# Pacing transfers and stages in the plan of a conv-scan-attention kernel on one core

## The chip, the cores and the metric

The kernel runs on one core of a Trainium2 chip. The core has five engines with a queue each, in which instructions run in order: PE (matmuls), DVE (VectorE), ACT (ScalarE), POOL (GpSimd) and SP (SyncE, which here issues all transfers). The metric is the device time of one execution in microseconds (us); lower is better.

## The reference, cut to what matters

Eight images of 384 channels and 32 x 32 pixels (1024 tokens) go through two layers. The first is a Mamba block, run forward and backward over the tokens, beside a local 3 x 3 convolution. The second is causal attention with 6 heads, and a feed-forward layer.

```python
# layer 0, per image; L = 1024 tokens, C = 384 channels, 16 states
u, z  = split(rmsnorm(x) @ in_proj)              # also with tokens reversed
u     = silu(causal_conv4(u) + b)
dt, Bm, Cm = split(u @ x_proj)
delta = softplus(dt @ dt_proj + dt_b)
h[t]  = exp(delta*A)[t] * h[t-1] + (delta*u)[t] * Bm[t]   # scan, C x 16 rows
y     = (sum over states of h*Cm + u*D) * silu(z)
x     = x + res * (scale * (y_fwd + y_bwd) @ out_proj + sigmoid(conv3x3(xn)) * xn)
# layer 1
t = t + attention(layernorm(t));  t = t + ffn(layernorm(t))
```

## The kernel before, in words

**Tiles.** The 384 x 16 scan rows of an image and a direction are cut into groups of 128 rows (8 channels x 16 states). With two directions that is 96 groups, so 96 scans a batch (one image) and 768 in all. A scan step (`group`) has these instructions: SP loads `dA` (512 KB, delta broadcast over the states), ACT takes its exponential (L999), PE spreads delta times u over the rows into a PSUM ring (L323, `ring<-du,dup`), DVE multiplies it with B in two halves (L1028), DVE runs the scan (L1034, `h<-dA,ring`), POOL multiplies h with C (L1038), PE sums over the states (`y<-h,sel`). There are six `dA` and six `h` buffers.

**Stages.** Around the scans of batch b stand the other stages of the neighbouring batches: `project` and `gates` (norm, in_proj; PROJECT), `prepare` (causal convolution and x_proj; CONV), `deltas` (softplus and the splitting of delta times u in three bf16 parts, 39 POOL operations of 1024 columns a batch, L794 and L903 to L918; DELTA), `local` (the 3 x 3 convolution; LOCAL), `finish` (out_proj, layer norm; OUTPUT), `attention` (ATTEND), and `forward` (feed-forward; FORWARD). Their tiles come from one pool of 26 buffers and a PSUM pool of four banks. They pass data by DRAM: `urd`, `xpd`, `ded`, `dusd`, `uzd`, `ygd`, `x1d`.

**Order.** Nothing is in the order of the source. Every operation is recorded in a `Plan` with an engine, a cost, what it reads and writes, and a priority `at`. `Plan.run` then goes through a model of the five engines in time: on each engine it takes, of the operations that could start first, the one with the lowest `at`. It writes out one fixed order for each engine. On the chip the engines follow this order, whatever the real times are.

An operation of a stage gets its `at` from the stage's stretch: `stretch` (L1397) turns, say, DELTA = (-0.82, -0.45) into a window of time around the start of its batch's scans, in units of PERIOD, and `Window` spreads the operations over it; transfers get MOVE less, evictions of PSUM EVICT less. An operation of a scan step is `placed` at its step's time with a lead: LOAD for the dA load, DECAY for the exponential, PRODUCTS for POOL's product, SUMS for PE's sums, PARTS for the load of delta times u. A lead is how much earlier, on the priority scale, the operation ranks than its scan. Operations that have an `at` of their own are `urgent`; in the scans these are all.

In the model a transfer takes its bytes over DMA_RATE, one after the other (`dma` is when the last is through), and DMA_LATENCY more. STAY lowers the `at` of ACT operations that need no change of ACT's function table. The choice:

```python
for t, o in cand:
    if t <= t0 + 0.05:
        a = o.at - (self.STAY if e == "ACT" and o.table in (None, table) else 0.0)
        k = (a, o.index)
```

Of the kernel before, what the change touches and what calls it, by code (L numbers as in the profile page):

```python
# [104 lines left out]
class Plan:  # L105
    LATENCY = 0.06
    SLACK = 0.3
    SWITCH = 1.3
    STAY = 0.0
    DMA_LATENCY, DMA_RATE = 2.5, 280e3  # L110

    def __init__(self, slots):
        self.ops, self.slots = [], slots
# [53 lines left out]
    def run(self):  # L167

        engines = ("PE", "ACT", "DVE", "POOL", "SP")
        free = {e: 0.0 for e in engines}  # L170
        ready = {e: [] for e in engines}
        dma = 0.0
        table = None
        slots = {k: [(0.0, i) for i in range(n)] for k, n in self.slots.items()}

        queue = {k: [] for k in slots}
        for o in self.ops:
            for v in o.allocs:
                if v.kind != "psm":
                    queue[v.kind].append((o.at, o.index, v))  # L180
                    o.waits += 1
        for q in queue.values():
            q.sort(key=lambda a: a[:2])
            q.reverse()
        owner = {}
        for o in self.ops:
            for v in o.allocs:
                owner[id(v)] = o

        def release(o, t):  # L190
            o.ready = max(o.ready, t)
            o.waits -= 1
            if o.waits == 0:
                ready[o.engine].append(o)

        def hand_out(kind):
            while queue[kind] and slots[kind]:
                v = queue[kind].pop()[2]
                t, v.slot = heapq.heappop(slots[kind])
                release(owner[id(v)], t)  # L200

        for o in self.ops:
            if o.waits == 0:
                ready[o.engine].append(o)
        for kind in queue:
            hand_out(kind)
        order = []

        def bank_time(o):

            need = {}
            for v in o.allocs:
                if v.kind == "psm":
                    need[v.kind] = need.get(v.kind, 0) + 1
            t = 0.0
            for k, n in need.items():
                if len(slots[k]) < n:
                    return None
                t = max(t, sorted(slots[k])[n - 1][0])
            return t  # L220

        total = len(self.ops)
        while len(order) < total:
            best = None
            for e in engines:
                cand = []
                for o in ready[e]:
                    t = o.ready
                    if o.allocs:
                        tb = bank_time(o)  # L230
                        if tb is None:
                            continue
                        t = max(t, tb)
                    cand.append((max(t, free[e]), o))
                if not cand:
                    continue
                t0 = min(c[0] for c in cand)

                pick, key = None, None
# [4 lines that stand above are left out]
                        if key is None or k < key:  # L244
                            pick, key, start = o, k, t
                if best is None or start < best[0]:
                    best = (start, e, pick)
            assert best is not None, "the slots do not suffice"
            start, e, o = best
            ready[e].remove(o)  # L250
            for v in o.allocs:
                if v.kind == "psm":
                    _, v.slot = heapq.heappop(slots[v.kind])
            cost = o.cost
            if e == "ACT" and o.table is not None and o.table != table:
                cost += self.SWITCH
                table = o.table
            free[e] = start + cost
            o.done = start + cost + self.LATENCY
            if e == "SP":  # L260
                dma = max(dma, start + cost) + o.nbytes / self.DMA_RATE
                o.done = dma + self.DMA_LATENCY
            order.append((start, len(order), o))
            for u in o.after:
                release(u, start)
            for u in o.users:
                release(u, (o.done if u.engine != e or e == "SP" else free[e]) + (0.0 if u.urgent or u.engine == e else self.SLACK))
            for v in o.vals:
                v.left -= 1
                v.end = max(v.end, o.done)  # L270
                if v.left == 0 and v.kind is not None:
                    heapq.heappush(slots[v.kind], (v.end, v.slot))
                    if v.kind != "psm":
                        hand_out(v.kind)
        order.sort(key=lambda a: a[:2])
        return [o for _, _, o in order]
# [3 lines left out]
def conv_attn_hybrid_kernel(  # L280
# [162 lines left out]

    EVICT, MOVE, SUMS, PRODUCTS, DECAY, LOAD, PARTS = 20.0, 15.0, 30.0, 20.0, 35.0, 45.0, 10.0

    CONV, DELTA, LOCAL, PROJECT = (-0.84, -0.78), (-0.82, -0.45), (-0.51, -0.36), (-1.28, -1.16)
    OUTPUT, ATTEND, FORWARD = (1.04, 1.12), (1.2, 1.85), (1.88, 1.97)

    class Window:

# [939 lines left out]

    PERIOD, HEAD = 475.0, 90.0

    def stretch(span, b):  # L1397
        return Window(span[0] * PERIOD, span[1] * PERIOD, HEAD + b * PERIOD)
# [117 lines left out]
```

## Time and profile before

| | |
|---|---|
| time, median of 3 runs | 4386.56 us (4378.64 to 4395.95) |
| the profiled execution | 4387.34 us, its span 4385.3 us |
| busy | PE 83%, DVE 78%, POOL 68%, ACT 66% of the span |
| DMA | 884.15 MB, mean 202 GB/s |
| table loads | 260, 333.6 us of ACT |
| granted PE clock, mean | 0.888 |

The time around the span is 2 us. Busy shares are averages over stages with different limits, and matmuls are pipelined, so a busy PE is not PE at its peak. "PE s L323" in a wait means: the instruction that wrote tile s, recorded at line 323 (the helper through which most matmuls go). In the prediction, batch n is the stretch from the first scan of image n to the first of image n + 1, and a block is an eighth of it, 12 scans.

### The profile page before, as it was taken

Reading aid. Unit: us, or ns where it says so; the run is one execution under the profiler, and the core shown is the slowest. Engines: PE = TensorE matmul, PEld = TensorE weight load, DVE = VectorE, ACT = ScalarE, POOL = GpSimd, SP = SyncE. Lnnn points to the kernel's source line nnn. Section 1 sums busy time; section 2 is a strip of 40 time slices with the busy share of each in tenths; the row PEclk is TensorE's granted clock in tenths of the full one; section 3 lists DMA queues with packets and bytes.
Section 4 is the critical chain, followed back from the end, with each engine's and each line's share of the span. In section 5 each row is a group of like instructions: output and inputs, shape, how many; then the busy total and the mean of one; then the engine's idle time right before and its main releaser. Section 6 shows DMA issues by size and latency. Waiting matters only on the chain. (4 is left out here: it accounts for less than half of the span.)

```text
span 4385.3 us, 55001 instructions
## 1 busy us (share of the span) xinstructions
PE 3655.8 (83%) x17970; PEld 1442.5 (33%) x17970; DVE 3432.0 (78%) x3661; ACT 2886.3 (66%) x4598; POOL 3000.9 (68%) x2370
## 2 busy tenths in 40 slices
PE   6476668789887899889898899878898888888998
PEld 2021112334233332334333332333323332343363
DVE  1676789879887899869996799879898699999422
ACT  4648436766677758767677767777578666665463
POOL 2967856987579865987569864897559875676231
PEclk8586679889998999889997999979998899999998
DMA  6798995687866788677876879677876757556200
GB/s 214 245 279 252 264 278 170 178 243 213 228 206 201 215 244 246 178 221 219 221 228 181 236 216 253 186 204 226 223 231 179 231 165 197 156 145 171 77 16 25
DMA packets 308918, 884.15 MB, mean 202 GB/s; under 512 B 39080, under 2 KB 92344, under 8 KB 308632
## 3 DMA queue, kind: packets, MB, share of 16 engines
q1 hardware_dynamic: 308632, 880.64, 69.6%
q8 instruction: 143, 2.34, 0.2%
q14 instruction: 143, 1.17, 0.1%
HBM read 709.03 MB, written 173.26 MB: 201 GB/s over the span
## 5 line engine op out<-in xcount | busy, mean ns | idle before, releaser
L1038 POOL TENSOR_TENSOR h<-h,bc 128x1024 f32<-128x1024 f32 x768 | 1810.2, 2362 | 899.2 <-DVE h L1034 735.5
L1034 DVE TENSOR_TENSOR_SCAN h<-dA,ring 128x1024 f32<-128x1024 f32 x768 | 1755.4, 2286 | 164.7 <-PE y L323 64.9
L1028 DVE TENSOR_TENSOR ring<-ring,bc 128x512 f32<-128x512 f32 x1536 | 1071.1, 697 | 331.8 <-PE ring L323 223.0
L999 ACT ACTIVATE dA<-dA,nA 128x1024 f32<-128x1024 f32 x768 | 870.9, 1147 | 584.3 <-DMA dA<-ded 540.6
L323 PE MATMUL ring<-du,dup 32*128 32x512 bf16 x1536 | 327.9, 418 | 404.1 <-DVE h L1034 385.9
L323 PE MATMUL y<-h,sel 128*32 128x512 f32 x3072 | 567.6, 688 | 26.3 <-POOL h L1038 23.2
L1197 DVE TENSOR_REDUCE mx<-s 128x1 f32<-128x512 f32 (+3 forms) x576 | 286.5, 544 | 214.5 <-PE s L323 214.5
L1204 ACT ACTIVATE p<-s,mx 128x512 f32<-128x512 f32 (+3 forms) x576 | 330.4, 579 | 130.6 <-DVE mx L1197 129.3
L1250 POOL TENSOR_SCALAR p<-p,den 128x512 f32<-128x512 f32 (+3 forms) x576 | 328.2, 588 | 113.5 <-DVE den L1243 107.5
L1257 PE MATMUL t<-ident,p 128*128 128x128 f32 x1728 | 304.4, 313 | 117.3 <-POOL p L1250 65.8
L323 PEld LDWEIGHTS <-dup 32*128 32x128 bf16 x1536 | 73.7, 92 | 944.1 <-DVE h L1034 831.7
L1452 ACT ACT_TABLE_LOAD x260 | 333.6, 1283 | 4.7
L1264 ACT COPY pT<-t 128x512 f32<-128x512 f32 (+3 forms) x576 | 253.0, 483 | 124.5 <-PE t L1257 121.8
L323 PE MATMUL s<-k,q 64*128 64x512 f32 (+3 forms) x1152 | 303.5, 579 | 32.5 <-ACT p L1204 30.8
L1257 PEld LDWEIGHTS t<-ident,p 128*128 128x128 f32 x1728 | 216.8, 157 | 269.5 <-POOL p L1250 130.3
L323 PE MATMUL pi<-xp,win 128*128 128x512 f32 x576 | 284.4, 617 | 9.8 <-ACT zt L730 5.7
L323 PE MATMUL pc<-pT,v 128*64 128x128 f32 x3456 | 267.9, 297 | 5.3 <-ACT pT L1264 4.6
L323 PEld LDWEIGHTS pc<-pT,v 128*64 128x64 f32 x3456 | 208.4, 147 | 99.1 <-issue 37.9
L918 POOL TENSOR_TENSOR u<-u,part 128x1024 f32<-128x1024 f32 x96 | 204.6, 2131 | 52.5 <-ACT part L910 52.5
L910 ACT CAST part<-u 128x1024 bf16<-128x1024 f32 x144 | 150.1, 1043 | 57.6 <-DMA dusd<-part 22.7
L323 PEld LDWEIGHTS y<-h,sel 128*32 128x32 f32 x3072 | 88.0, 115 | 289.6 <-issue 146.9
L323 PE MATMUL pg<-yg,wout 128*128 128x512 f32 x288 | 155.8, 658 | 21.0 <-DMA yg<-ygd 18.4
(184 smaller groups left out, 4814.8 us busy)
## 6 DMA issues: line engine op xcount, KB each, us to landing
dA<-ded SPq DMA_DIRECT2D x768, 512.0 KB
ct<-urd SPq DMA_DIRECT2D x96, 513.5 KB
du<-dusd SPq DMA_DIRECT2D x96, 512.0 KB
xs<-xpd SPq DMA_DIRECT2D x96, 432.8 KB
dusd<-part SPq DMA_DIRECT2D x288, 128.0 KB
ded<-de SPq DMA_DIRECT2D x48, 512.0 KB
uz<-uzd SPq DMA_DIRECT2D x48, 512.0 KB
bc<-bcd SPq DMA_DIRECT2D x32, 512.0 KB
```

Source lines behind the costliest of these rows:

```text
L323: return nc.tensor.matmul(out_, lhsT=lhsT, rhs=rhs, start=first, stop=last)
L918: "POOL", pool(L), lambda part=part: nc.gpsimd.tensor_sub(du.t, du.t, part.t), [part], [du]
L999: "ACT", act(L) + 0.1, lambda: nc.scalar.activation(dA.t, dA.t, AF.Exp, scale=nA.t[:, g : g + 1]),
L1028: uses("DVE", nc.vector.tensor_mul(to, to, bc.t[:, 0, half(hf)]), [bank_of(v)])
L1034: i = nc.vector.tensor_tensor_scan(h.t[:, rev], dA.t[:, rev], t[:, rev], 0.0, ALU.mult, ALU.add)
L1038: op("POOL", pool(L), lambda: nc.gpsimd.tensor_mul(h.t, h.t, bc.t[:, 1]), [(bc, 1)], [h], at=at - PRODUCTS)
L1197: lambda sc=sc, g=g, w=k1 - k0, hh=hh: nc.vector.tensor_reduce(mx.t[:, g, hh : hh + 1], sc[hh].t[:, 0:w], AX.X, ALU.max, negate=True), [sc ...
L1204: nc.scalar.activation(ps[hh].t[:, k0:k1], sc[hh].t[:, 0 : k1 - k0], AF.Exp, bias=mx.t[:, g, hh : hh + 1], accum_out=den.t[:, g, hh : hh + 1],
L1250: nc.gpsimd.tensor_scalar(t, t, den.t[:, g, hh : hh + 1], 1.0, ALU.mult, ALU.mult)
L1257: nc.tensor.transpose(t.t[:, j * P - k0 : (j + 1) * P - k0], ps[hh].t[:, j * P : (j + 1) * P], ident)
L1264: nc.scalar.copy(pT[hh].t[:, k0 // P : k1 // P, :].rearrange("p j t -> p (j t)"), t.t[:, 0 : k1 - k0])
L1452: nc.scalar.preload_act_table_set(table)
```

## The change

It changes no computation and no tile. In the model it adds a gate: a transfer that isn't urgent may start only when the transfers under way have no more than BACKLOG = 4 us left. The model's rate of DMA goes from 280 to 262 GB/s, and ACT now prefers by 10 us to stay with its function table (LANDING is 0 and has no effect). The leads PRODUCTS, DECAY, LOAD and PARTS get smaller, PRODUCTS below zero, so that a product ranks after its scan's own time. The stretches of the stages and PERIOD are set anew. Lines of the kernel after line 262 move by four.

```diff
     SWITCH = 1.3
-    STAY = 0.0
-    DMA_LATENCY, DMA_RATE = 2.5, 280e3
+    STAY = 10.0
+    BACKLOG = 4.0
+    LANDING = 0.0
+    DMA_LATENCY, DMA_RATE = 2.5, 262e3
...
                         t = max(t, tb)
+                    if e == "SP" and not o.urgent:
+                        t = max(t, dma - self.BACKLOG)
                     cand.append((max(t, free[e]), o))
...
                 dma = max(dma, start + cost) + o.nbytes / self.DMA_RATE
-                o.done = dma + self.DMA_LATENCY
+                o.done = dma + self.DMA_LATENCY + self.LANDING
...
-    EVICT, MOVE, SUMS, PRODUCTS, DECAY, LOAD, PARTS = 20.0, 15.0, 30.0, 20.0, 35.0, 45.0, 10.0
-
-    CONV, DELTA, LOCAL, PROJECT = (-0.84, -0.78), (-0.82, -0.45), (-0.51, -0.36), (-1.28, -1.16)
-    OUTPUT, ATTEND, FORWARD = (1.04, 1.12), (1.2, 1.85), (1.88, 1.97)
+    EVICT, MOVE, SUMS, PRODUCTS, DECAY, LOAD, PARTS = 20.0, 15.0, 30.0, -10.0, 20.0, 15.0, 5.0
+
+    CONV, DELTA, LOCAL, PROJECT = (-0.93, -0.84), (-0.86, -0.39), (-0.41, -0.29), (-1.31, -1.16)
+    OUTPUT, ATTEND, FORWARD = (1.04, 1.22), (1.23, 1.78), (1.88, 1.97)
...
-    PERIOD, HEAD = 475.0, 90.0
+    PERIOD, HEAD = 420.0, 90.0
```

## The prediction

> **What bounds the kernel now.** I read the page first, then the windows of one batch, then the waits. The busy shares and the two costliest groups of the page:
>
> ```profile
> PE 3655.8 (83%) x17970; PEld 1442.5 (33%) x17970; DVE 3432.0 (78%) x3661; ACT 2886.3 (66%) x4598; POOL 3000.9 (68%) x2370
> ...
> L1038 POOL TENSOR_TENSOR h<-h,bc 128x1024 f32<-128x1024 f32 x768 | 1810.2, 2362 | 899.2 <-DVE h L1034 735.5
> L1034 DVE TENSOR_TENSOR_SCAN h<-dA,ring 128x1024 f32<-128x1024 f32 x768 | 1755.4, 2286 | 164.7 <-PE y L323 64.9
> ```
>
> No engine is full on average, so the averages decide nothing. The 768 scans on DVE are the kernel's clock: one scan and the two products with B before it (L1028, 697 ns each) cost 2.286 + 2 x 0.697 = 3.68 us, and every scan is followed by one product with C on POOL (L1038, 2.36 us). From the scans' start times the span divides into 138.3 us before the first scan, eight batches of 96 scans (494.9, 479.8, 504.2, 505.9, 505.7, 502.3, 517.7, and 445.0 to the end of the last scan), and 291.4 us after it. Batches 2 to 6 repeat one order, so I look at batch 3, cut into eight blocks of 12 scans. These are the windows of the blocks (busy us and instructions of each engine, granted clock, DMA share, GB/s):
>
> ```profile
> core 0: us, PE busy (x) PEld busy (x) DVE busy (x) ACT busy (x) POOL busy (x), PEclk, DMA share, GB/s
> 1617.00:1680.00 63.00, 55.59 (x204) 17.88 (x201) 55.79 (x57) 40.40 (x47) 30.06 (x14) 0.97 0.83 226
> 1680.00:1740.00 60.00, 55.24 (x238) 15.90 (x238) 56.77 (x59) 48.19 (x57) 30.29 (x14) 1.00 0.95 290
> 1740.00:1789.00 49.00, 45.49 (x219) 18.62 (x213) 43.96 (x38) 39.05 (x51) 35.71 (x16) 1.00 0.55 160
> 1789.00:1858.00 69.00, 57.45 (x282) 26.96 (x280) 51.60 (x57) 54.66 (x93) 68.24 (x48) 0.78 0.63 179
> 1858.00:1943.00 85.00, 65.95 (x380) 26.94 (x381) 55.57 (x66) 60.83 (x109) 76.46 (x65) 0.82 0.72 209
> 1943.00:2012.00 69.00, 60.23 (x396) 27.19 (x395) 58.32 (x71) 53.40 (x97) 57.07 (x62) 0.85 0.80 236
> 2012.00:2071.00 59.00, 55.66 (x328) 24.61 (x326) 55.52 (x63) 40.24 (x83) 40.85 (x46) 1.00 0.67 200
> 2071.00:2123.00 52.00, 48.31 (x224) 19.38 (x226) 48.69 (x47) 30.46 (x48) 34.99 (x33) 1.00 0.80 231
> ```
>
> The reader is to see two regimes. In blocks 2, 7 and 8 DVE is busy 93 to 95%: DVE is the bound. In blocks 4 to 6 DVE falls to 75, 65 and 85% while POOL has 99, 90 and 83%: POOL is the bound. What a DVE wait looks like there, the waits of block 5 alone:
>
> ```profile
> DVE mx L1197 <- PE s L323: 14.2, 1, 14.2
> DVE h L1034 <- PE y L323: 4.7, 1, 4.7
> DVE fac L1235 <- POOL fac L1232: 3.8, 1, 3.8
> ```
>
> PE is named, but PE's sums (y) wait for POOL's products, and whatever stands behind them on PE (the scores s) waits too. PE itself isn't full: its matmuls of a batch, each at the spacing that saturated stretches show (430 ns for a pass of 512 fp32 columns), make about 345 of 506 us.
>
> **What the Trainium skill says.** "DMA: Bandwidth & Descriptors" (Queues, rings and completion order; Anatomy of one DMA) says that DMA engines don't wait on semaphores: the issuing sequencer waits before dispatch. So a transfer that must wait holds up all transfers behind it on SP. The trace agrees: SP's queue waits 1405.1 us for scans to free a dA buffer. "ScalarE: Activation LUTs" (What ACT_TABLE_LOAD costs) gives about 1283 ns for a table load; the 260 loads here have a mean of 1283 ns. "Perfetto Trace Analysis" (Optimization Strategy) reads consistent gaps as a possible lack of buffers; here the gap of blocks 4 to 6 repeats in each batch, and h has six buffers.
>
> **The change, part by part.** It adds and removes no work but table loads: the changed program has the same instructions except 251 table loads for 261 (the opening one included). 10 x 1.283 = 13 us of ACT, which has 138 us of slack in each batch (367 of 506 busy): costed at nothing. All else is order. So I gave each instruction of the new order the duration that the same instruction had in this profile, and summed between scans (POOL: between its products). Per batch the sums stay (DVE 443, POOL 382, ACT 402 to 400). Block by block, us, batch 3:
>
> ```
> block          1     2     3     4     5     6     7     8
> measured      62.6  59.8  49.7  68.7  84.7  69.5  58.4  52.4
> DVE  before   57.5  59.3  44.8  53.0  57.8  62.1  57.7  50.4
> POOL before   29.6  29.6  43.1 100.6  57.1  45.4  40.1  36.1
> DVE  after    56.0  53.2  52.5  52.8  55.0  58.4  62.9  51.9
> POOL after    29.6  32.0  63.8  75.8  45.1  59.2  38.8  37.3
> MB   before   14.0  16.1  10.0  12.1  15.2  16.8  13.2  11.9
> MB   after    15.1  13.1  12.6  11.3  11.3  12.9  16.9  15.8
> ```
>
> POOL's peak is the delta stage. Block 4 has 12 products (28.5), 23 delta operations (52.7) and softmax scaling (19.4); in the new order the 39 delta operations of a batch spread over 1, 13, 13, 6 and 6 in blocks 2 to 6 (before: 6, 23 and 10 in blocks 3 to 5). A rule follows from before: **DVE loses about POOL's largest surplus over it in a run of blocks.** Block 4: 100.6 - 53.0 = 47.6; by half blocks, scans 30 to 48: 127.1 - 75.6 = 51.5. Measured: blocks 4 to 6 took 222.9 us for 172.9 of DVE work, a loss of 50.0. After: blocks 3 and 4, 139.6 - 105.3 = 34.3; by half blocks, scans 30 to 66, 201.6 - 158.4 = 43.2. The gain is 8 to 13 us; I take 10. Batches 2 to 6: **-50 us**. What is late next is DVE itself (443 of work in about 496), and ACT in block 5 (67.1 of work).
>
> Batch 1: surplus before, blocks 3 to 5, 193.6 - 155.6 = 38.0 (measured loss of blocks 3 to 6: 40.3); after, 204.9 - 162.4 = 42.5, by half blocks 49.8. **+8 us**.
>
> Batch 0 mixes two bounds: DMA runs at 0.90 with 264 GB/s, and DVE loses 111 us, of which POOL's surplus explains 39 (blocks 1 and 2: 10; 4 and 5: 29). In the order, dA loads stand in its second half only 0.5 to 3.5 scans ahead of their scan; in the new one 3 to 5. 134.6 MB between its first and last dA load become 126.5; batch 1 takes the rest. Against that, POOL's surplus grows to 29 (block 1, 74.0 - 44.9) and 60 (block 5, 114.2 - 54.3). So 384 of DVE work + 89 + about 12 left of other waits = 485: **-10 us**, with -35 and +20 as ends.
>
> Head: the compute engines' order up to the first scan is the same but for two POOL operations. On SP, ten small weight loads (wqkv_2, bvc, w_fc1, w_p1, kr2) move from ahead of the convolution's loads to behind them: 10 issues of 0.5 to 1.2 us, about 7 us; PE waits 19.1 us for wc there. The loads' own 6.9 MB hide some. **-5 us**. The selection of kr2 on POOL waits longer then, but POOL idled 24.6 us after it.
>
> Batch 7 (428 of DVE work in both) and the tail (DVE 78 in both, ACT 162 to 159, PE a few us less): 0 and **-3**.
>
> The gate itself (BACKLOG): a transfer outside the scans is put after more dA loads, and each of these waits for a scan. Behind it wait its stage's first matmul or activation. The trace can't show that delay; above, the earlier windows (CONV from -0.93 instead of -0.84) should pay for it. I bound it by +20 us a batch (the 19.1 us that PE waits for wc in the head) and, since a dA load that finds a shorter queue can also land earlier, by a gain of 6 (the first rival); I take 0. The later priority of POOL's products (PRODUCTS) is in the block sums; its side effect, that sums stand up to six scans behind in more places, costs nothing as long as POOL is the bound there.
>
> Sum: -50 + 8 - 10 - 5 - 3 = -60, against the profiled execution's 4387.3 us: 4327. The median, 4386.6, is 0.7 lower; I say **4326**.
>
> **Rivals.**
> - *The transfers come free* (13%): dA loads are on time in batch 0 (the 111 us of loss become 75) and POOL's surplus costs 16 a batch less. -36 - 80 + 8 - 8: about 4270. For it: the leads of the loads in the new order. Against: block 5 of batch 0 needs 114 us of POOL whatever DMA does.
> - *The stall moves* (18%): products put behind softmax scaling wait for ACT and DVE on the in-order POOL queue, POOL idles in blocks 3 to 6 as it does now (34 us between 1740 and 2012, though 246 of work stand there) and the loss stays at 50. -50 is gone: about 4377.
> - *DMA becomes the bound between batches* (17%), slower: blocks 7, 8 and 1 now carry 39.1 MB in 173.4 us, 225 GB/s; in the new order 47.8 MB in about 176, 272 GB/s. If the queue gives only 245 there, they take 195, 19 us more, and every scan waits for its dA: 5 x (19 - 10) + 8 - 10 - 8, about 4422. It decides below 47.8 MB / 186 us = 257 GB/s. Against it: block 2 now moves 290 GB/s at a share of 0.95 with DVE 95% busy. For it: batch 0 kept no more than 264.
>
> **How the numbers follow.** The forecast (own range 4295 to 4360) has 52%, the rivals 13, 18 and 17. A measurement of this kernel tells about 0.5% (22 us) from no change. Faster by more: 52 + 13 = 0.65; within: 0.18; slower: 0.17. The range 4262 to 4402 takes in the second rival, the ends of batch 0 and half of the slow one.
>
> **What would show it.** Right: in the windows of batch 3 the time of blocks 4 to 6 falls from 223 to about 200 and block 3 grows to some 62; no window has POOL at 0.99 with DVE below 0.7; batches 2 to 6 take about 496; the first scan starts near 133; 250 table loads. The forecast is wrong if blocks 3 to 6 together stay at 272, if ACT's waits on dA's DMA grow beyond 540.6 us with DVE waiting behind them, or if block 5 of batch 0 takes over 130 us.

## The result, and the profile after

| | before | after |
|---|---|---|
| median of 4 runs, us | 4385.08 (4378.64 to 4395.95) | 4320.97 (4314.89 to 4327.89) |
| profiled execution; its span, us | 4387.34; 4385.3 | 4314.89; 4313.2 |
| granted PE clock, mean | 0.888 | 0.90 |

The ratio is 0.9852 (95% interval 0.9823 to 0.988): **faster by 1.5%**, 64 us by the medians. The page of after, its busy shares and the same two groups:

```profile
PE 3641.6 (84%) x17970; PEld 1454.5 (34%) x17970; DVE 3426.9 (79%) x3661; ACT 2871.3 (67%) x4588; POOL 3003.6 (70%) x2370
...
L1042 POOL TENSOR_TENSOR h<-h,bc 128x1024 f32<-128x1024 f32 x768 | 1808.3, 2364 | 887.0 <-DVE h L1038 746.0
L1038 DVE TENSOR_TENSOR_SCAN h<-dA,ring 128x1024 f32<-128x1024 f32 x768 | 1755.3, 2286 | 271.7 <-PE y L327 130.7
```

Work and durations are the same (2286 ns a scan, 2362 and 2364 a product); the shares rose because the span fell. The scan even waits longer for PE's sums (130.7 us against 64.9). From the scans' start times:

| stretch, us | head | b0 | b1 | b2 | b3 | b4 | b5 | b6 | b7 | tail |
|---|---|---|---|---|---|---|---|---|---|---|
| before | 138.3 | 494.9 | 479.8 | 504.2 | 505.9 | 505.7 | 502.3 | 517.7 | 445.0 | 291.4 |
| after | 135.7 | 503.9 | 491.9 | 486.6 | 497.3 | 485.4 | 489.9 | 489.4 | 443.8 | 289.2 |

Batches 2 to 6 gained 87.2 us, batches 0 and 1 lost 21.1, the rest gained 6. The windows of after's batch 3, the same eight blocks of 12 scans (us, busy us and instructions of each engine, granted clock, DMA share, GB/s):

```profile
1618.00:1676.00 58.00, 52.62 (x187) 16.03 (x185) 53.86 (x54) 39.40 (x46) 28.50 (x13) 1.00 1.03 252
1676.00:1738.00 62.00, 56.41 (x257) 15.11 (x256) 51.71 (x50) 52.58 (x59) 30.94 (x15) 0.94 0.97 269
1738.00:1793.00 55.00, 49.73 (x198) 20.71 (x197) 50.85 (x52) 43.01 (x61) 48.40 (x21) 0.98 0.63 187
1793.00:1851.00 58.00, 53.91 (x271) 24.77 (x270) 50.89 (x54) 45.53 (x83) 56.36 (x42) 0.79 0.59 183
1851.00:1921.00 70.00, 60.70 (x384) 33.46 (x382) 52.35 (x61) 51.51 (x97) 67.88 (x61) 0.89 0.55 163
1921.00:1982.00 61.00, 48.72 (x318) 20.15 (x318) 55.34 (x65) 48.90 (x95) 58.35 (x63) 0.86 0.93 261
1982.00:2052.00 70.00, 59.67 (x354) 24.11 (x355) 60.37 (x71) 47.65 (x88) 45.92 (x48) 0.93 0.86 237
2052.00:2115.00 63.00, 59.62 (x289) 24.76 (x289) 49.81 (x49) 34.99 (x58) 37.01 (x34) 1.00 0.73 218
```

Blocks 4 to 6 took 189 us (before 223), but blocks 7 and 8 took 133 (before 111): DVE is now busy 86 and 79% where it had 94% in both. So a large gain in the middle of the batch is partly given back at its end. In batch 4, scans 24 to 72 went from 272.3 to 240.9 us and scans 72 to 96 from 109.8 to 128.4.

### The profile page after: what moved, and what is told of

The parts are those of the page before. It is cut to its first block, busy times and chain, and to the rows that moved or that the text cites. A ratio compares the mean times of both kernels' runs of the same rounds, so it can differ in the third digit from the quotient of the medians.

```text
span 4313.2 us, 54972 instructions
## 1 busy us (share of the span) xinstructions
PE 3641.6 (84%) x17970; PEld 1454.5 (34%) x17970; DVE 3426.9 (79%) x3661; ACT 2871.3 (67%) x4588; POOL 3003.6 (70%) x2370
## 5 line engine op out<-in xcount | busy, mean ns | idle before, releaser
L1042 POOL TENSOR_TENSOR h<-h,bc 128x1024 f32<-128x1024 f32 x768 | 1808.3, 2364 | 887.0 <-DVE h L1038 746.0
L1038 DVE TENSOR_TENSOR_SCAN h<-dA,ring 128x1024 f32<-128x1024 f32 x768 | 1755.3, 2286 | 271.7 <-PE y L327 130.7
L1003 ACT ACTIVATE dA<-dA,nA 128x1024 f32<-128x1024 f32 x768 | 873.6, 1147 | 493.3 <-DMA dA<-ded 443.3
L1254 POOL TENSOR_SCALAR p<-p,den 128x512 f32<-128x512 f32 (+3 forms) x576 | 328.8, 591 | 83.5 <-DVE den L1247 72.0
L1261 PEld LDWEIGHTS t<-ident,p 128*128 128x128 f32 x1728 | 227.2, 161 | 212.9 <-POOL p L1254 114.3
L327 PEld LDWEIGHTS s<-k,q 64*128 64x128 f32 x1152 | 120.1, 202 | 177.4 <-ACT p L1208 65.8
```

The lines of the kernel that those rows point to most:

```text
L327: return nc.tensor.matmul(out_, lhsT=lhsT, rhs=rhs, start=first, stop=last)
L1003: "ACT", act(L) + 0.1, lambda: nc.scalar.activation(dA.t, dA.t, AF.Exp, scale=nA.t[:, g : g + 1]),
L1038: i = nc.vector.tensor_tensor_scan(h.t[:, rev], dA.t[:, rev], t[:, rev], 0.0, ALU.mult, ALU.add)
L1042: op("POOL", pool(L), lambda: nc.gpsimd.tensor_mul(h.t, h.t, bc.t[:, 1]), [(bc, 1)], [h], at=at - PRODUCTS)
L1254: nc.gpsimd.tensor_scalar(t, t, den.t[:, g, hh : hh + 1], 1.0, ALU.mult, ALU.mult)
L1261: nc.tensor.transpose(t.t[:, j * P - k0 : (j + 1) * P - k0], ps[hh].t[:, j * P : (j + 1) * P], ident)
```

## The experiments

Twelve kernels, in the order in which they ran. Each ratio is to runs of before taken beside that kernel (their medians lie between 4383.76 and 4390.18 us), and after itself was measured only at the start, at 0.9852 [0.9823, 0.988]. **Theory 1** is the prediction's: POOL's surplus over DVE holds the scans up, and the new stretches spread it. Its rivals give the gain to the gate with the rate, or to the leads alone.

**e1_old_stretches.** After, with the stretches of before.

```diff
-    CONV, DELTA, LOCAL, PROJECT = (-0.93, -0.84), (-0.86, -0.39), (-0.41, -0.29), (-1.31, -1.16)
-    OUTPUT, ATTEND, FORWARD = (1.04, 1.22), (1.23, 1.78), (1.88, 1.97)
+    CONV, DELTA, LOCAL, PROJECT = (-0.84, -0.78), (-0.82, -0.45), (-0.51, -0.36), (-1.28, -1.16)
+    OUTPUT, ATTEND, FORWARD = (1.04, 1.12), (1.2, 1.85), (1.88, 1.97)
-    PERIOD, HEAD = 420.0, 90.0
+    PERIOD, HEAD = 475.0, 90.0
```

> The changed kernel with the stretches of the stages and PERIOD = 475 of the kernel before; gate, rate, STAY and leads stay new. Theory 1 (the new stretches spread the delta stage over POOL's queue, and POOL's surplus over DVE in a run of scans is what DVE loses): in this order the surplus of batches 2 to 6 is about 64 us each, against 51 before and 43 in the changed kernel, so it is slower than the kernel before, about 4440 us. Rival G (the gate on transfers makes the gain): it keeps the gate, so about 4325 to 4340. Rival L (the smaller leads make it): the same, about 4325.

Measured 4425.06 us, ratio to before 1.0084 [1.0056, 1.0112]. Without the new stretches the change is a loss; gate, rate, STAY and leads together do not carry it. Theory 1 came near with its 4440, but not for its reason: batches 2 to 6, in which it saw the loss, are 8 us shorter than in before (2528 against 2536), and the loss stands in batch 0 (7 us), batch 1 (13), batch 7 (8) and the tail (18).

**e2_no_gate.** After, without the gate and at the old rate.

```diff
-    DMA_LATENCY, DMA_RATE = 2.5, 262e3
+    DMA_LATENCY, DMA_RATE = 2.5, 280e3
-                        t = max(t, dma - self.BACKLOG)
+                        t = max(t, dma - 1e9)
```

> The changed kernel without the gate (transfers outside the scans are never held back in the plan) and with the model's old rate of 280 GB/s; stretches, PERIOD, STAY and leads stay new. Theory 1: surplus of batches 2 to 6 about 41 us, of batch 1 32 instead of 54, of batch 0 50 instead of 60, so as fast as the changed kernel or up to 30 us faster, 4290 to 4325. Rival G: the gain goes, about 4385. Rival L: about 4320.

Measured 4354.81 us, 0.9915 [0.9896, 0.9934]: nearly half of the gain is gone. Theory 1, which gave gate and rate nothing, fails here.

**e3_old_leads.** After, with PRODUCTS, DECAY, LOAD, PARTS of before.

```diff
-    EVICT, MOVE, SUMS, PRODUCTS, DECAY, LOAD, PARTS = 20.0, 15.0, 30.0, -10.0, 20.0, 15.0, 5.0
+    EVICT, MOVE, SUMS, PRODUCTS, DECAY, LOAD, PARTS = 20.0, 15.0, 30.0, 20.0, 35.0, 45.0, 10.0
```

> The changed kernel with the leads of the kernel before (PRODUCTS 20, DECAY 35, LOAD 45, PARTS 10). Theory 1: surplus of batches 2 to 6 about 36 us instead of 43, batch 1 44 instead of 54, so 4270 to 4320. Rival G: about 4320, since the gate is kept. Rival L: the gain goes, about 4385.

Measured 4362.58 us, 0.9935 [0.991, 0.9961]. The leads are needed too; theory 1 had expected the old ones to be as good or better.

**e4_stretches_leads.** Before, with the new stretches, PERIOD and leads alone (gate, rate and STAY as before).

```diff
-    EVICT, MOVE, SUMS, PRODUCTS, DECAY, LOAD, PARTS = 20.0, 15.0, 30.0, 20.0, 35.0, 45.0, 10.0
+    EVICT, MOVE, SUMS, PRODUCTS, DECAY, LOAD, PARTS = 20.0, 15.0, 30.0, -10.0, 20.0, 15.0, 5.0
...
-    CONV, DELTA, LOCAL, PROJECT = (-0.84, -0.78), (-0.82, -0.45), (-0.51, -0.36), (-1.28, -1.16)
-    OUTPUT, ATTEND, FORWARD = (1.04, 1.12), (1.2, 1.85), (1.88, 1.97)
+    CONV, DELTA, LOCAL, PROJECT = (-0.93, -0.84), (-0.86, -0.39), (-0.41, -0.29), (-1.31, -1.16)
+    OUTPUT, ATTEND, FORWARD = (1.04, 1.22), (1.23, 1.78), (1.88, 1.97)
...
-    PERIOD, HEAD = 475.0, 90.0
+    PERIOD, HEAD = 420.0, 90.0
```

> The kernel before with the new stretches, PERIOD and leads; no gate, the old rate of 280 GB/s, STAY 0. Theory 1: surplus like the version without the gate (41 in batches 2 to 6, 32 in batch 1), so 4290 to 4325. Rival G: about 4385. If staying with ACT's table mattered (10 table loads of 1.283 us), it would be some 13 us slower than the version without the gate alone.

Measured 4401.68 us, 1.0021 [1.0009, 1.0033]: no gain from these two. It differs from e2 by STAY alone, and that difference of 47 us lies largely in the tail, 314.5 us here and 286.6 in e2. It is not the table loads: e4 has 240 of them, e2 and after 250.

**e5_before_short_subs, e6_after_short_subs.** The order untouched, 12 of POOL's subtractions a batch (L918 in before, 2.13 us each) done on one column of 1024 (the rest of the splitting is left out), which takes 25 us a batch off POOL where its surplus is.

```diff
-                    "POOL", pool(L), lambda part=part: nc.gpsimd.tensor_sub(du.t, du.t, part.t), [part], [du]
+                    "POOL", pool(L), lambda part=part: nc.gpsimd.tensor_sub(du.t[:, 0:1], du.t[:, 0:1], part.t[:, 0:1]), [part], [du]
```

> The kernel before in the same order, with POOL's subtraction that splits delta times u in three parts (two for each channel block and direction, 12 a batch, 2.13 us each) done on one column of 1024, so that the parts are wrong: 12 x 2.0 = 25 us less of POOL a batch and nothing else. Theory 1 (POOL's surplus over DVE in a run of scans is what DVE loses): the surplus of batches 2 to 6 goes from 51 to 35, of batch 0 from 37 to 20, of batch 1 from 38 to 17, 120 us in all, so 4265 to 4300. Rival R (POOL is busy there but something else, transfers or PE's order, holds DVE): less than 20 us gained, 4365 or more.

> The changed kernel in the same order with the same cut (the parts are wrong). Theory 1: POOL still bounds scans 30 to 66 of each batch in the changed kernel (surplus 43, 23 with the cut; 329 to 191 in all), so 4180 to 4230. If the change had taken POOL off the path, little would come: over 4290.

Measured on before 4384.38 us, 0.9988 [0.997, 1.0006], no clear gain where some 90 to 120 us had been expected; on after, in two runs, 4300.33 us, 0.9805 [0.9759, 0.9852], some 20 us under after where 90 to 140 had been expected, and its interval touches that of after. **The surplus rule falls.** How it could fall is seen when DVE's loss is looked at scan by scan: most of it sits in a few single steps. In batch 4 of before a step takes some 4 us, but that of scan 37 takes 19.0, 51 takes 14.9, 53 takes 21.5 and 63 takes 12.6. The windows of before around the first three:

```profile
2301.00:2320.00 19.00, 14.73 (x67) 6.33 (x67) 7.77 (x13) 16.53 (x28) 18.92 (x13) 0.72 0.50 160
2380.00:2395.00 15.00, 10.06 (x59) 6.02 (x58) 5.09 (x9) 12.58 (x24) 14.58 (x21) 0.61 0.39 99
2400.00:2422.00 22.00, 16.34 (x88) 4.97 (x90) 6.68 (x11) 10.69 (x21) 16.54 (x11) 0.77 0.87 237
```

and of e5 at the same scans:

```profile
2305.00:2322.00 17.00, 14.08 (x64) 5.79 (x62) 7.34 (x12) 15.61 (x26) 16.09 (x13) 0.68 0.57 174
2381.00:2395.00 14.00, 8.07 (x58) 3.94 (x58) 5.21 (x9) 12.58 (x25) 13.19 (x23) 0.74 0.41 100
2401.00:2422.00 21.00, 16.48 (x80) 4.78 (x84) 6.26 (x10) 10.48 (x21) 12.14 (x10) 0.67 0.87 245
```

POOL is busy all through the first step of before, but when its work there becomes 2.8 us shorter the step shrinks by 1 or 2; in the third POOL drops from 16.5 to 12.1 and the step stays. So a busy engine beside a stall need not be its cause: at most a part of the first step was POOL's work.

**e7_after_short_in_proj.** After, order untouched, two of the three passes of in_proj's matmuls (`pi`) cut to 32 of 512 columns, since the stalls of after's scans 80 to 90 stand beside them.

```diff
-                            lambda p=p, m=m, hf=hf, c=c: (grid(p.t), win.t[:, c, chans(m)], inside(xp[c].t, hf)),
+                            lambda p=p, m=m, hf=hf, c=c: (
+                                grid(p.t)[:, 0 : RH if c == 0 else 1], win.t[:, c, chans(m)],
+                                inside(xp[c].t, hf)[:, 0 : RH if c == 0 else 1],
+                            ),
```

> The changed kernel with two of the three matmuls of each in_proj sum done on 32 of 512 columns (the sums are wrong): 24 a batch, 24 x 0.8 = 19 us less of PE a batch, most of it in blocks 7 and 8, in the same order. If PE bounds block 8 now (38 of its 53 us of matmul lie in scans 84 to 90, 72 with 94% busy PE): block 8 goes from 63.5 to about 54, and the kernel to 4260 to 4285. Rival D (transfers of 47.8 MB in blocks 7, 8 and 1 make dA late): no change, 4310 or more.

Measured in two runs 4306.52 us, 0.9819 [0.9773, 0.9866], about 15 under after, and not to be told from it. PE's work in scans 72 to 96 of batch 4 fell from 117.3 to 110.1 us and the stretch did not shorten (128.4 and 130.4). Seven us less of PE's work bought nothing there. The test is weaker than planned: 19 us a batch were to go, most of them at this end.

**e8_old_rate.** After, gate kept, rate 280.

```diff
-    DMA_LATENCY, DMA_RATE = 2.5, 262e3
+    DMA_LATENCY, DMA_RATE = 2.5, 280e3
```

> The changed kernel with only the model's rate of DMA back at 280 GB/s; the gate stays. By theory 1 its order has a smaller surplus everywhere (batches 2 to 6: 37 instead of 43; batch 1: 41 instead of 54) and less PE work in the last blocks, so 4260 to 4310. If the gate and the lower rate together make the gain, it lies between the changed kernel and the one without the gate, 4325 to 4355.

Measured 4344.48 us, 0.9891 [0.9849, 0.9933], and e2 had 0.9915 [0.9896, 0.9934]: by the medians the gate without the lower rate brings 10 us, and by the intervals that is not told from nothing. It runs from 4324.9 to 4353.47 us in four runs, and the profiled one is the slowest.

**Theory 2, and e9 to e11.** The timeline of before at scan 53 (start us, us, engine, line, operation; in brackets the idle time before it and what ended it):

```profile
2400.26 2.28 DVE L1034 TENSOR_TENSOR_SCAN h<-dA,ring 128x1024 f32<-128x1024 f32 x1
...
2406.34 0.67 PE L1257 MATMUL t<-ident,p 128*128 128x128 f32 x2 [2.52 <-POOL p L1250]
...
2409.65 0.18 PEld L323 LDWEIGHTS pw<-xs,wl__15509 96*32 96x32 f32 x2 [1.39 <-DMA xs<-xpd]
...
2414.09 0.14 PEld L323 LDWEIGHTS pw<-xs,wl__15509 96*32 96x32 f32 x2 [4.25 <-DMA xs<-xpd]
...
2418.36 1.65 PE L323 MATMUL s<-k,q 64*128 64x384 f32 x4
...
2420.27 1.02 DVE L1197 TENSOR_REDUCE mx<-s 128x1 f32<-128x384 f32 x2 [13.38 <-PE s L323]
...
2421.79 2.29 DVE L1034 TENSOR_TENSOR_SCAN h<-dA,ring 128x1024 f32<-128x1024 f32 x1 [0.50 <-issue]
```

DVE idles 13.38 us in front of a maximum that needs PE's scores s. The scores are not late by themselves: they stand on PE's in-order queue behind matmuls `pw` of the local convolution, whose data xs are still under way, and behind transposes that wait for POOL's p. Theory 2 was that such late operands on PE's queue make the long steps. e9 takes away the one: its local convolution leaves out the loaded data and reads a resident weight tile. e10 and e11 take away the other: attention's transposes leave out p and read the identity.

```diff
-                            xg = xs[g].t.rearrange("p (h w) -> p h w", w=WP)
+                            xg = wl.t.rearrange("p a d m -> p (a d m)").rearrange("p (h w) -> p h w", w=W)
...
-                                t.t[:, j * P - k0 : (j + 1) * P - k0], ps[hh].t[:, j * P : (j + 1) * P], ident
+                                t.t[:, j * P - k0 : (j + 1) * P - k0], ident, ident
```

> The kernel before, with its order of instructions untouched; only the matmuls pw of the local convolution read, in place of the loaded tile xs, the weight tile wl, which is in its buffer long before (part left out: the local convolution's data; same matmuls, same sizes, the loads of xs still issued). It takes away what TensorE waits 54.2 us for in the page of before (22 waits, 4 to 7 us each in the scan 53 of every batch). Queue theory (DVE is lost in a few single steps in which TensorE's in-order queue stands at one matmul whose operand is late): the step from scan 53 to 54 falls from 21.5 us to 8 to 14, some 10 us a batch in seven batches, 4300 to 4330. Rival, that the next late operand in the same queue (the transposes t waiting for GpSimd's p) takes the place at once: 4370 to 4390. Rival of the sums (POOL's or PE's total of work): 4380 to 4390.

> The kernel before, order untouched; only attention's transposes t read the resident identity in place of p (part left out: the transposed weights of attention; same instructions, same sizes; the exponentials and GpSimd's scaling of p still run). TensorE no longer waits for GpSimd's p: 65.8 us in front of matmuls and 130.3 in front of weight loads in before. Queue theory: the steps from scan 37 (19.0 us), 51 (14.9) and part of 53 fall to 8 to 12, some 15 us a batch in batches 2 to 6 and some in 0 and 1 and in the tail: 4270 to 4320. Rival, the late transfers alone: 4370 to 4390. Rival, that these waits lie beside DVE's own chain of maximum and reciprocal (mx, den, fac), which stays: 4350 to 4380.

> The kernel after with the same edit as the run before this one: attention's transposes read the resident identity (same part left out). Queue theory: what is left in after (16.6 us in scan 53, and 8 to 9 us in the scans 80, 85, 87, 89 in which attention meets the next batch's input projection) falls by some 8 us a batch, and the tail's attention is shorter: 4230 to 4280; the gain on after is smaller than the same edit's gain on before, since the change has already taken part of these waits. If it gains as much as on before, the change did not work through them. Rival, that DVE's own chain sets scans 80 to 91: 4300 to 4320.

| run | measured, us | ratio to before | the step it aimed at, batch 4 |
|---|---|---|---|
| e9 (before) | 4365.28 | 0.9953 [0.9937, 0.9969] | scan 53: 21.5 to 16.7 us |
| e10 (before) | 4373.1 | 0.9973 [0.996, 0.9987] | scan 37: 19.0 to 17.8; 51: 14.9 to 15.1 |
| e11 (after) | 4306.3 | 0.9808 [0.9764, 0.9853] | scan 53: 16.6 to 14.4; 85, 87, 89 unchanged |

All three missed the numbers of theory 2. e9 gains some 20 us, a third of what it should, and the step stops at 16.7 us. e10 gains some 12, e11 can't be told from after. e10 and e11 lie in the range of a rival that no run takes apart: that DVE's own chain of maximum and reciprocal sets these steps. This is how e9's step looks with every operand of the local convolution in place:

```profile
2402.84 0.82 PE L1257 MATMUL t<-ident,p 128*128 128x128 f32 x2 [4.09 <-POOL p L1250]
...
2409.86 0.20 PEld L323 LDWEIGHTS y<-h,sel 128*32 128x32 f32 x8 [0.20 <-issue]
2409.86 1.02 DVE L1197 TENSOR_REDUCE mx<-s 128x1 f32<-128x384 f32 x2 [7.91 <-PE s L323]
...
2411.90 2.29 DVE L1034 TENSOR_TENSOR_SCAN h<-dA,ring 128x1024 f32<-128x1024 f32 x1 [1.01 <-issue]
```

PE is busy 12.6 of its 17 us. Between one scan and the next the order has put that much on PE's queue, ahead of the sums y and the scores that DVE needs, and the wait for POOL's p (4.09 us) is most of the rest. The late xs is gone, and the step is still long. Is it long in the order itself?

**e12_after_norm_on_act.** After, computing all of it; the scaling of p leaves POOL for ScalarE at the same places of the order.

```diff
-                        nc.gpsimd.tensor_scalar(t, t, den.t[:, g, hh : hh + 1], 1.0, ALU.mult, ALU.mult)
+                        nc.scalar.activation(t, t, AF.Copy, scale=den.t[:, g, hh : hh + 1])
```

> The kernel after, computing all of it: attention's scaling of p by 1/den is issued on ScalarE in place of GpSimd, at the same places of the order. 576 instructions of 571 ns mean (328.8 us) leave GpSimd, where each stands behind products of 2.4 us, and come to ScalarE, about 480 to 580 ns each, some 40 us a batch on an engine that is 67% busy. Queue theory: TensorE's wait for p falls from 152 us (37.7 and 114.3) to under 80, gain of some 5 us a batch: 4270 to 4300. Rival, that ScalarE's queue becomes the late one (the exponentials dA and the casts behind the scalings): 4330 to 4400.

Measured 4377.2 us, 0.9986 [0.9973, 0.9998], as its rival had it: nearly the whole gain of the change is gone. The waits of PE and of its weight loads for p in after:

```profile
PE t L1261 <- POOL p L1254: 37.7, 31, 3.8
...
PEld t L1261 <- POOL p L1254: 114.3, 132, 4.1
```

and in e12:

```profile
PE t L1261 <- ACT p L1254: 71.1, 73, 3.4
...
PEld t L1261 <- ACT p L1254: 149.8, 163, 3.7
```

They grew from 152 to 221 us instead of falling. The plan had reckoned with POOL for this work and had filled ScalarE's queue without it; that this is why the waits grew is argued, not shown.

## What the runs say together: the order's own times

After the last run I set the trace beside the order itself. As the kernel is built, `Plan.run` gives each instruction a start in its own model; I wrote out those starts of the 768 scans. They are the kernel's estimates from its own constants, no times of the chip, and are used here only to ask which long steps the order contains and which the chip adds. For the long steps of batch 4 (us):

| step of scan | before: plan | before: chip | e9: chip | after: plan | after: chip |
|---|---|---|---|---|---|
| 37 | 19.9 | 19.0 | 19.0 | 6.1 | 5.7 |
| 51 | 14.1 | 14.9 | 13.8 | 7.9 | 7.3 |
| 53 | 16.2 | 21.5 | 16.7 | 16.0 | 16.6 |
| 63 | under 6 | 12.6 | 10.7 | under 6 | 4.0 |
| 85, 87, 89 | under 6 | 4.0, 4.0, 5.0 | 4.0, 4.0, 5.0 | 9.2, 9.7, 8.9 | 8.4, 8.9, 8.3 |

Most long steps are in the order. e9, which makes the data of the local convolution always ready, brings scan 53 nearly down to its planned length and no further; in e10 the steps that are as long as planned hardly changed. Scan 63 of before is one that the chip adds. There ACT's own queue waits twice for a transfer of dA (1.88 and 1.79 us), the exponential p behind it comes late, and the scores after it too:

```profile
2466.21 1.15 ACT L999 ACTIVATE dA<-dA,nA 128x1024 f32<-128x1024 f32 x1 [1.79 <-DMA dA<-ded]
...
2468.08 0.79 PE L323 MATMUL s<-k,q 64*128 64x128 f32 x2 [4.06 <-ACT p L1204]
...
2469.13 0.49 DVE L1197 TENSOR_REDUCE mx<-s 128x1 f32<-128x128 f32 x2 [4.16 <-PE s L323]
```

Then the sums over batches 2 to 6, for each kernel with another order (plan and chip in us; the last column is ACT's wait for dA's transfer in the whole run, from the waits):

| kernel | gate, rate | STAY | stretches | leads | plan | chip | chip - plan | ACT waits for dA |
|---|---|---|---|---|---|---|---|---|
| before | none, 280 | 0 | old | old | 2451 | 2536 | 85 | 540.6 |
| e4 | none, 280 | 0 | new | new | 2430 | 2515 | 85 | 580.0 |
| e2 | none, 280 | 10 | new | new | 2426 | 2499 | 73 | 522.4 |
| e8 | gate, 280 | 10 | new | new | 2427 | 2497 | 70 | 562.6 |
| after | gate, 262 | 10 | new | new | 2421 | 2449 | 28 | 443.3 |
| e1 | gate, 262 | 10 | old | new | 2492 | 2528 | 36 | 464.1 |
| e3 | gate, 262 | 10 | new | old | 2468 | 2499 | 31 | 463.4 |

The table falls into two. With the gate and the lower rate together, the chip takes 28 to 36 us more than the plan; in the other four it takes 70 to 85 more, whatever the stretches and the leads are. The stretches and the leads in turn set the length of the plan (2421 to 2492). ACT's wait for dA's transfers goes with the groups (443 to 464 us against 522 to 580), not with the length: in before and in after

```profile
ACT dA L999 <- DMA dA<-ded: 540.6, 285, 9.3
...
ACT dA L1003 <- DMA dA<-ded: 443.3, 246, 8.4
```

and in e8, the same kernel as after but for the rate,

```profile
ACT dA L1003 <- DMA dA<-ded: 562.6, 298, 8.5
```

PE's wait for xs doesn't follow the groups: 54.2 us in before and 16.0 in after, but 31.6 and 35.9 in e3 and e1, and 25.1 and 27.0 in e2 and e8.

One doubt is that the plans come from two models, and that a plan made with the slower rate leaves less to exceed. So I kept each order as it stands and went through it again in the kernel's model with the other rate, without the gate (these are estimates too). The orders made for 262 hardly change at 280: after's batches 2 to 6 stay at 2420. The orders made for 280 can't bear 262: before becomes 2498, e4 2479, e2 2479 and e8 2482, which leaves 15 to 38 us of chip minus plan in all seven. So the difference between the groups is about what a slower transfer does to an order that was planned for a faster one. For the whole span 262 takes off too much (it leaves -10 to 12 us for these four, 38 to 53 for the others); a rate of some 266 to 270 fits both better.

For the whole span, each kernel by its own model: plan 4289.9 to 4273.0, chip minus plan 95.4 to 40.2. **Of the 72 us between the two profiled executions, 17 are a shorter order and some 55 an order that the chip keeps to better.** Of the 17, the middle of the batch gains 19 in batch 4's plan (scans 24 to 72: 260.3 to 241.1) and its end gives back 18.5 (scans 72 to 96: 110.2 to 128.7); batch 1's plan grows by 14.4. e2, without gate and lower rate, shows the larger part by itself: its plan, 4272.5, is as long as after's, and its span is 40 us longer.

What is argued and what is shown: that the pair of gate and rate separates the two groups is shown by seven orders, one profiled execution each; a single one of these differences is good to some 10 us (orders that didn't change, such as before and e5, differ by that), and the profiled execution is the fastest of after's four but the slowest of e8's and of e3's. With each kernel's median in place of it, the whole span exceeds the plan by 25 to 57 us with gate and rate and by 80 to 99 in the others, so the groups stay apart. That transfers on time are the link is shown for scan 53 by e9; elsewhere it rests on the waits that go with it and on the orders at the other rate. Not run: the lower rate without the gate, so their shares are open (the model, an estimate, gives that order 2443 us in batches 2 to 6 against after's 2421); gate and rate on before's stretches and leads. Open too is why the chip takes 17 to 31 us more than the plan in batch 0 of every kernel, with the gate or without; DMA is there at a share of 0.90 in before and 0.85 in after.

## Why the prediction was right, point by point

The forecast, 4326, met 4321, inside its own range. Its sum does not stand as it was made.

- **Batches 2 to 6, -50: measured -87.** The rule failed: "DVE loses about POOL's largest surplus over it in a run of blocks". e5 and e6 took 25 us of POOL's work a batch away, and little moved. It probably fitted before because the delta stage and the long steps lie in the same scans. The line that the prediction read as PE's sums waiting for POOL (DVE's 14.2 us for the scores s) is scan 53: in batch 4 the scores stood there behind the local convolution and its late xs. The Trainium skill, "Perfetto Trace Analysis" (Optimization Strategy), says that a gap which repeats can mean too few buffers; no run here changed their number, but for scan 53 e9 and the plan name other causes. Blocks 4 to 6 fell from 223 to 189 (said: about 200), block 3 grew to 55 only (said: 62).
- **The gate at 0, with -6 to +20 a batch: the term that was mis-sized.** Together with the rate it is worth 57 of the 87 (85 - 28, by the plans), 11 a batch, beyond the lower bound. I priced the gate as a delay of single transfers and gave the rate no term at all. What the pair does is to keep transfers from being planned into a queue that can't carry them: in the kernel's model before's order is 47 us longer at 262 than at 280 (2498 against 2451), and after's is not. The Trainium skill, "DMA: Bandwidth & Descriptors" (Anatomy of one DMA), which the prediction cites, says that the issuing sequencer does the waiting, before it dispatches. SP's queue fits that; its first wait in before and in after is

```profile
SPq L424 <- DVE h L1034: 1405.1, 499, 8.1
...
SPq L428 <- DVE h L1038: 1744.2, 594, 7.7
```

  so SP stands ready for a buffer for 339 us more. That goes with the gate (1702.3 in e1, 1795.7 in e3), but it is not yet the gain: e8, with the gate alone, has 1647.8.
- **Blocks 7, 8 and 1, nothing: from 173 to 192 us in batch 3.** This is the size and the place of the third rival (19 us), but hardly its mechanism: in batch 4 the plan of scans 72 to 96 is 18.5 longer, and the chip keeps to it. The surplus of one engine over another had no term for work that stands in front of a scan on PE's queue.
- **Batch 1, +8: measured +12,** right in sign, by the failed rule; in the plan it is +14. By half blocks the surplus of the new order is 54, not the 49.8 that stands in the prediction, so the rule asked for up to +16.
- **Batch 0, -10: measured +9,** inside its ends. Its plan hardly moved (+1.4). The dA loads further ahead of their scans brought nothing, and block 1, to which the rule gave a loss of 29, took 50.3 us. Block 5 took 114.6, the number of POOL's sum of 114, but POOL is busy for only 91 of it, and with less work for POOL (e6) it took 112.1. The plan has 113.0.
- **Head -5, batch 7 0, tail -3: measured -2.6, -1.2, -2.2.** The first scan came at 135.7; e6, e7, e11 and e12, which have after's order, had 133.3 to 134.3. The tail's 2 hides two terms that I didn't see and that cancel: with the new stretches and without STAY it is 23 longer (e4, 314.5), and STAY takes that back (e2, 286.6).
- **Table loads, 10 fewer, nothing:** 250 of them, as said.

Of the rivals, "transfers come free" came nearest to the mechanism (ACT waits 443.3 us for dA where it waited 540.6), in the wrong place: batches 2 to 6, not batch 0. The two errors of the sum, 37 us too little in batches 2 to 6 and 23 in batches 0 and 1, had opposite signs; that the total was within 5 us is luck.

## What to carry to other kernels

In a statically ordered kernel, look for the loss step by step before summing engines: a window in which an engine is 99% busy doesn't make it the bound, and taking a part of its work away there is the quick test (here a tenth, 24 of 238 us between scans 24 and 72, shortened that stretch by 6 us and the kernel by nothing clear). Then ask of each long step whether the order contains it or the chip adds it, since the two need different cures: other windows and leads for the first, a model of the transfers that is true (a rate the queue really gives, and no transfer planned into a queue already full) for the second. And don't move work to another engine behind the planner's back: where the order is tight, a place that it didn't plan cost 56 us here.

## What the runs showed of the hardware

- **What a full DMA queue gives depends on the mix.** At a share of 1.03 it moved 252 GB/s (block 1 of after's batch 3), at 0.97 it moved 269, at 1.02 in e9's scan 53 it moved 282, and in block 2 of before's batch 3 290 at 0.95; over the whole of batch 0 of before it was 264 at 0.90. A single rate in a plan is a compromise.
- **ScalarE was not quicker than GpSimd at the small scaling:** 336.0 us for the 576 in e12, 328.8 on GpSimd in after.
- **The granted clock didn't follow PE's load in one direction.** It was 0.61 to 0.77 in the three long steps of before, where PE is busy 67 to 78%, and 1.00 in blocks 2, 7 and 8 of before's batch 3 at 92 to 94%. But block 4 of after's batch 3 had 0.79 with PE busy for 93%, so neither a low load nor a high one explains a low clock here.
